# The order of score products inside a round: two halves of the array take the round's tiles in opposite order

## The chip, the cores and the metric

The kernel runs on one core of a Trainium2 chip. The metric is device time in microseconds from the start to the end of one launch: 2753.59 us, the median of three runs (2750.57 to 2754.35). A profile of one further execution, with a record of every instruction, goes with it. In it PE is the matrix engine TensorE, PEld its weight loads, DVE VectorE, ACT ScalarE, POOL GpSimd and SP the engine that issues transfers.

## What is computed

A pre-norm transformer layer on x of shape (4, 1024, 1024) in f32: attention with 32 heads of 32 elements and rotary positions, then a top-1 mixture of eight low-rank adapters. Only the scores matter here:

```
q = rotary(layernorm(x) @ wq);  k = rotary(layernorm(x) @ wk);  v = layernorm(x) @ wv
scores = einsum('bqhd,bkhd->bhqk', q, k) / sqrt(32)      # causal
out    = einsum('bhqk,bkhd->bqhd', softmax(scores), v)
x = x + out @ wo
x = x + adapter(layernorm(x))
```

Each score is a sum over the 32 elements of a head; because of the causal mask a block of queries needs only the keys up to itself.

## The kernel before

**Units.** Work goes through 32 units, one for each batch (4) and group of four heads (8). For a unit the queries and keys of its four heads lie in `qT` and `kT` with the 128 rows being head by element, so head h occupies rows 32h to 32h+31.

**Tiles of queries and rounds.** The 1024 queries of a unit are cut into 16 tiles t = 0 to 15 of 64 queries. Tile t needs the first (t+1)*64 keys. The tiles are computed in nine rounds, listed in `SLOTS` (lines 26 to 38) as (tile, first key, last key); two more entries of that list ("second", "first") are the places where the probabilities of a finished half are multiplied with the values. Four rounds hold one tile (15, 14, 13, 12), three hold two (7 and 6; 11 and a piece of 8; 10 and the rest of 8), one holds three (5, 4, 3) and one holds four (2, 1, 0 and 9).

**A round.** `score_round` (lines 393 to 423) fills one scores buffer `sc` of 128 rows by 4 heads by 512 columns; there is a single such buffer, and the value products use it too. The 128 rows are four strips of 32: strip i = 2*half + odd, where `half` says which 32 of the tile's 64 queries, and `odd` whether the strip takes the even or the odd blocks of 32 keys. Two strips together hold one set of queries, so a tile with K keys takes w = K/2 columns. Every (strip, head) pair is one product: 32 rows of one head as contraction, 32 queries as stationary operand, w keys as moving operand. It therefore uses one of the 16 squares of 32 by 32 of the matrix array: head h picks the array's rows, strip i the array's columns. A tile takes 16 products, one on each square, and the next tile of the round takes the same squares again.

The widths w by round are: 256+224; 192+160+128; 96+64+32+320; 512; 480; 448; 416; 384+128; 352+160.

**The order before.** For each tile of the round in the order of `SLOTS`, strips 0 to 3, and in a strip heads 0 to 3 (loops of lines 399, 402 and 404). So all 16 products of one tile stand ahead of the 16 of the next.

**After the products.** Lines 415 to 423: ScalarE copies each tile's scores into the probabilities' block `pr` (L417), GpSimd adds the causal mask on the diagonal (L420), VectorE finds the maxima (L438) and joins two strips (L459), ScalarE exponentiates (L467), VectorE transposes (L492). The value products `av` (L573) follow on eight squares of 64 by 32.

**What stands around a round.** The order of TensorE's instructions is written by hand (a manual schedule). Between rounds the kernel takes steps from a list `todo`: the projections of the next unit (`chain`, L313, matmuls of 128 by 128 by 512), and, from the second batch on, the output projection and the adapter of the batch before (L690, L712, L751). How many steps follow each round is set by costs and by `LENGTHS`, none of which the change touches.

Of the kernel before, what the change touches and what calls it, by code (L numbers as in the profile page):

```python
# [14 lines left out]
P = 128  # L15
# [4 lines left out]
SQ = 32  # L20
# [51 lines left out]
def tile_preln_attn_then_top1_lora(  # L72
# [78 lines left out]
    for i in range(P // SQ):  # L151
        half, odd = divmod(i, 2)
# [233 lines left out]
    def place(u, t):  # L386
        blk = t // QT
        if (u, blk) not in blocks:
            blocks[u, blk] = big.tile([P, HG, WIDTH[blk]], F32, tag=f"prob{blk}", name=f"pr_{u}_{blk}")
        at = (t % QT) * APART[blk]  # L390
        return blocks[u, blk][:, :, at : at + (t + 1) * SQ]

    def score_round(u, pieces):
        sc = ps_s.tile([P, HG, HALF], F32, tag="s", name=f"s_{u}_{pieces[0][0]}_{pieces[0][1]}")
        of_q = qTs[u].rearrange("p (j k) -> p j k", k=SQ)
        of_k = kTs[u].rearrange("p (j c k) -> p c j k", c=2, k=SQ)
        at = 0
        spans = []
        for t, k0, k1 in pieces:
            w = (k1 - k0) // 2  # L400

            for i in range(P // SQ):
                half, odd = divmod(i, 2)
                for h in range(HG):
                    rows = slice(h * HD, (h + 1) * HD)
                    nc.tensor.matmul(  # L406
                        sc[i * SQ : (i + 1) * SQ, h, at : at + w].rearrange("p (j k) -> p j k", k=SQ),
                        lhsT=of_q[rows, 2 * t + half],
                        rhs=of_k[rows, odd, k0 // (2 * SQ) : k1 // (2 * SQ)],
                        start=True,  # L410
                        stop=True,
                    )
            spans.append((t, k0 // 2, w, at))
            at += w
        for t, k0, w, at in spans:
            pr = places[u, t] if (u, t) in places else places.setdefault((u, t), place(u, t))
            nc.scalar.copy(pr[:, :, k0 : k0 + w], sc[:, :, at : at + w])  # L417
            if k0 + w == (t + 1) * SQ:
                diagonal = pr[:, :, t * SQ : (t + 1) * SQ]
                nc.gpsimd.tensor_tensor(  # L420
                    diagonal, diagonal, causal_sb.unsqueeze(1).to_broadcast([P, HG, SQ]), ALU.add
                )
                ended.append(t)
# [583 lines left out]
    for u, (b, g) in enumerate(units):  # L1007
# [10 lines left out]
        for r, pieces in enumerate(SLOTS):  # L1018
# [20 lines left out]
            else:  # L1039
                release_exps()  # L1040
                turn_probabilities()
                if second < r < first_:
                    join_sums(u, 0)
                score_round(u, pieces)
                if r == second - 1 and u:
                    while any((u - 1, t) in places for t in range(QT, 2 * QT)):
# [40 lines left out]
    left = sum(s.cost for s in todo) - APART_BY  # L1087
# [55 lines left out]
```

## Time and profile before

| what | value |
|---|---|
| median of three runs | 2753.59 us |
| the profiled execution, its time | 2747.7 us |
| its span, first to last instruction | 2745.9 us |
| mean granted TensorE clock | 0.998 |
| L406, score products: records, busy | 17408, 393.0 us |
| L406, weight loads: records, busy | 17408, 187.2 us |
| L573, value products: busy | 273.2 us |
| L313, projections pq, pk, pv: busy | 476.8, 475.9, 484.1 us |
| L417, ScalarE's copies of scores: busy, idle before | 525.3, 492.3 us |

How to read it: busy time is the union of the instructions of a group. Every f32 product leaves two matmul records and two weight-load records, so 8704 score products give 17408 of each. The length of a single matmul record reaches from its start to a modelled end; the products of one round overlap, so their lengths add up to far more than their busy time. "Idle before" is the time in which the group's engine stood still before its instructions.

### The profile page before, as it was taken

The page shows a single profiled execution, that of the slowest core. Times are in us where ns is not written, and L with a number is a line of the kernel's source. Part 1 is how long each engine was busy: PE and PEld are TensorE (multiplying, and loading weights), DVE is VectorE, ACT ScalarE, POOL GpSimd, SP SyncE. Part 2 cuts the span into 40 slices and gives each one's busy share as a digit, 9 for nine tenths or more (in the row PEclk, how much of TensorE's full clock was granted, in tenths as well). Part 3 has the DMA queues.
Part 4 walks back from the last instruction along what each step waited for, and adds up shares of the span by engine and source line. Part 5 has one row for each costly group of instructions (what it writes and reads, how often), then busy time and mean ns, then how long its engine had stood idle before and what let it go on. Part 6 is the DMA issues. An engine that isn't in the chain of part 4 may idle for free.

```text
span 2745.9 us, 84082 instructions
## 1 busy us (share of the span) xinstructions
PE 2682.2 (98%) x35328; PEld 1322.0 (48%) x35328; DVE 2126.7 (77%) x4198; ACT 1755.0 (64%) x5033; POOL 638.1 (23%) x900
## 2 busy tenths in 40 slices
PE   8999999899999999989999999998999999999998
PEld 5444444444445444445444454444544444544445
DVE  4888889887777877887777778788777777778655
ACT  2877777876666676666666666666566666666521
POOL 2222223222222222222222222222222222222000
PEclk9999999999999999999999999999999999999999
DMA  3222232325444455551654444565255544446421
GB/s 118 52 56 56 56 94 56 78 56 150 131 135 114 121 141 142 151 171 43 175 145 122 135 110 121 149 165 146 63 157 150 138 128 128 115 119 196 129 67 55
DMA packets 448012, 317.86 MB, mean 116 GB/s; under 512 B 150289, under 2 KB 371729, under 8 KB 447633
## 3 DMA queue, kind: packets, MB, share of 16 engines
q1 hardware_dynamic: 447632, 312.47, 41.6%
q8 instruction: 278, 4.55, 0.7%
q14 instruction: 102, 0.83, 0.1%
HBM read 262.59 MB, written 49.81 MB: 114 GB/s over the span
## 4 chain that ended last, share of the span: by engine, by line
PE 80%; DVE 14%; ACT 2%; DMA 1%; POOL 1%; issue 1%; SPq 0%; POOLq 0%; DVEq 0%; ACTq 0%
PE po L690 14%; PE pq L313 14%; PE pk L313 13%; PE pv L313 12%; PE s L406 11%; PE av L573 9%; DVE top L438 4%; DVE pr L492 4%; PE ph L712 2%; PE pf L751 2%; DMA chunk<-in_wo 1%; DVE both L459 1%; PE pr L547 1%; ACT pr L417 1%; PE pt_f L198 1%
## 5 line engine op out<-in xcount | busy, mean ns | idle before, releaser
L467 ACT ACTIVATE pr<-pr,both 128x256 f32<-128x256 f32 (+15 forms) x2048 | 1045.1, 519 | 58.0 <-DVE both L459 57.9
L438 DVE TENSOR_REDUCE top<-pr 128x2 f32<-128x960 f32 (+15 forms) x768 | 651.1, 894 | 251.5 <-POOL pr L420 250.9
L417 ACT COPY pr<-s 128x640 f32<-128x640 f32 (+14 forms) x544 | 525.3, 1017 | 492.3 <-PE s L406 491.7
L492 DVE STREAM_TRANSPOSE pr<-pr 128x1024 f32<-128x1024 f32 (+11 forms) x768 | 664.3, 907 | 33.3 <-ACT pr L467 30.1
L420 POOL TENSOR_TENSOR pr<-pr,causal_sb 128x128 f32<-128x128 f32 x512 | 238.0, 472 | 1070.6 <-ACT pr L417 1062.4
L313 PE MATMUL pv<-xnT,wv 128*128 128x512 f32 x1024 | 484.1, 600 | 0.0
L313 PE MATMUL pq<-xnT,wq 128*128 128x512 f32 x1008 | 476.8, 600 | 0.6 <-ACT xnT L200 0.6
L313 PE MATMUL pk<-xnT,wk 128*128 128x512 f32 x1008 | 475.9, 601 | 0.0
L406 PE MATMUL s<-kT,qT 32*32 32x256 f32 (+4 forms) x17408 | 393.0, 385 | 10.7 <-ACT pr L417 7.2
L467 ACT ACTIVATION_READ_ACCUMULATOR pr<-pr,both 128x1 f32 x2048 | 400.8, 196 | 0.0
L690 PE MATMUL po<-chunk,attn 128*128 128x512 f32 x736 | 376.3, 597 | 4.0 <-DMA chunk<-in_wo 4.0
L406 PEld LDWEIGHTS s<-kT,qT 32*32 32x32 f32 x17408 | 187.2, 103 | 267.2 <-issue 101.8
L313 PEld LDWEIGHTS pk<-xnT,wk 128*128 128x128 f32 x1008 | 181.3, 190 | 234.8 <-issue 234.6
L313 PEld LDWEIGHTS pq<-xnT,wq 128*128 128x128 f32 x1008 | 182.6, 191 | 224.0 <-issue 221.8
L313 PEld LDWEIGHTS pv<-xnT,wv 128*128 128x128 f32 x1024 | 185.7, 190 | 217.2 <-issue 212.9
L573 PE MATMUL av<-pr,vals 64*32 64x256 f32 (+3 forms) x12288 | 273.2, 320 | 11.7 <-DVE pr L492 11.6
L573 PEld LDWEIGHTS av<-pr,vals 64*32 64x32 f32 x12288 | 215.5, 106 | 119.9 <-issue 54.5
L459 DVE TENSOR_TENSOR both<-top 32x4 f32<-32x4 f32 (+3 forms) x1152 | 213.4, 185 | 23.7
L690 PEld LDWEIGHTS po<-chunk,attn 128*128 128x128 f32 x736 | 135.2, 190 | 168.0 <-issue 149.6
L548 ACT COPY by<-pr 128x512 f32<-128x512 f32 x64 | 37.5, 586 | 260.5 <-PE pr L547 260.5
L593 DVE TENSOR_TENSOR at<-av,by 128x256 f32<-128x256 f32 x128 | 48.1, 417 | 158.1 <-ACT by L548 158.0
L690 PE MATMUL po<-wo,attn 128*128 128x512 f32 x256 | 116.7, 597 | 0.0
(87 smaller groups left out, 1705.8 us busy)
## 6 DMA issues: line engine op xcount, KB each, us to landing
chunk<-in_wo SPq DMA_DIRECT2D x368, 256.0 KB, 3.6
vals<-vd SPq DMA_DIRECT2D x256, 128.0 KB, 4.5
x<-in_x SPq DMA_DIRECT2D x58, 512.0 KB, 6.0
wq<-in_wq SPq DMA_DIRECT2D x32, 512.0 KB, 4.0
wk<-in_wk SPq DMA_DIRECT2D x32, 512.0 KB, 4.0
wv<-in_wv SPq DMA_DIRECT2D x32, 512.0 KB, 4.2
vd<-vT SPq DMA_DIRECT2D x128, 128.0 KB, 4.8
out_y<-x SPq DMA_DIRECT2D x32, 512.0 KB, 2.8
```

The costliest lines, as they stand in the source:

```text
L313: nc.tensor.matmul(at["p"], lhsT=wt[:, c, :], rhs=xnTs[b, tb][:, c, :], start=(c == 0), stop=(c == NC - 1),)
L406: nc.tensor.matmul(sc[i * SQ : (i + 1) * SQ, h, at : at + w].rearrange("p (j k) -> p j k", k=SQ), lhsT=of_q[rows, 2 * t + half], rhs=of_k[ ...
L417: nc.scalar.copy(pr[:, :, k0 : k0 + w], sc[:, :, at : at + w])
L420: nc.gpsimd.tensor_tensor(diagonal, diagonal, causal_sb.unsqueeze(1).to_broadcast([P, HG, SQ]), ALU.add)
L438: nc.vector.tensor_reduce(top[:, k, h : h + step], places[u, t][:, h : h + step, :], AX.X, ALU.max, negate=True,)
L459: nc.vector.tensor_tensor(dst[rows], src[rows], src[other], op)
L467: nc.scalar.activation(pr[:, h, :], pr[:, h, :], AF.Exp, bias=tops[u, t][:, h : h + 1], accum_out=dens[u, t // QT][:, t % QT, h : h + 1],)
L492: nc.vector.transpose(pr, pr)
L573: nc.tensor.matmul(avs[half][h * HD : (h + 1) * HD, t0:, :], lhsT=v[rows, j, h * HD : (h + 1) * HD], rhs=rhs, start=(j == 0), stop=(j == n ...
L690: nc.tensor.matmul(st["po"], lhsT=lhsT, rhs=rhs, start=(c == start), stop=(c == stop))
L712: nc.tensor.matmul(ph, lhsT=st["ynT"][:, c, :], rhs=w[:, c - i * RA, :], start=(c == 0), stop=(c == NC - 1),)
L751: nc.tensor.matmul(pf, lhsT=st["whT"], rhs=rhs, start=True, stop=True)
```

## The change

The products of a round are the same; their order is another. The array's columns are taken as two halves, half 0 (strips 0 and 1) and half 1 (strips 2 and 3). Half 0 has a list of the round's tiles from the widest to the narrowest, half 1 from the narrowest to the widest. The code takes eight products at a time (two strips by four heads) from one of the two lists: from the half whose count of columns so far, plus 64 for each group taken, is the smaller one; half 0 at a tie. A round of 384+128 so becomes: 384 on half 0, 128 on half 1, 384 on half 1, 128 on half 0.

Where each tile's columns stand in `sc`, the copies after the products and their order remain. The slice of keys is written in another way, for the same keys (k0 and w now count half-columns).

```diff
         for t, k0, k1 in pieces:
             w = (k1 - k0) // 2
-
-            for i in range(P // SQ):
-                half, odd = divmod(i, 2)
+            spans.append((t, k0 // 2, w, at))
+            at += w
+
+
+        left = [sorted(spans, key=lambda p: -p[2]), sorted(spans, key=lambda p: p[2])]
+        busy = [0, 0]
+        while left[0] or left[1]:
+            half = 0 if left[0] and (not left[1] or busy[0] <= busy[1]) else 1
+            t, k0, w, at = left[half].pop(0)
+            busy[half] += w + 2 * SQ
+            for odd in range(2):
+                i = 2 * half + odd
                 for h in range(HG):
                     rows = slice(h * HD, (h + 1) * HD)
                     nc.tensor.matmul(
                         sc[i * SQ : (i + 1) * SQ, h, at : at + w].rearrange("p (j k) -> p j k", k=SQ),
                         lhsT=of_q[rows, 2 * t + half],
-                        rhs=of_k[rows, odd, k0 // (2 * SQ) : k1 // (2 * SQ)],
+                        rhs=of_k[rows, odd, k0 // SQ : (k0 + w) // SQ],
                         start=True,
                         stop=True,
                     )
-            spans.append((t, k0 // 2, w, at))
-            at += w
```

The groups of eight come out in this order (width, half):

| round | order of groups |
|---|---|
| 256+224 | 256 h0, 224 h1, 256 h1, 224 h0 |
| 192+160+128 | 192 h0, 128 h1, 160 h1, 160 h0, 192 h1, 128 h0 |
| 96+64+32+320 | 320 h0, 32 h1, 64 h1, 96 h1, 96 h0, 320 h1, 64 h0, 32 h0 |
| one tile | h0, h1 |
| 384+128 | 384 h0, 128 h1, 384 h1, 128 h0 |
| 352+160 | 352 h0, 160 h1, 352 h1, 160 h0 |

## The prediction

> **What bounds the kernel now.** I read the page's engine shares first, then its chain of waits, then the group that the change touches, then single rounds in the timeline.
>
> ```profile
> PE 2682.2 (98%) x35328; PEld 1322.0 (48%) x35328; DVE 2126.7 (77%) x4198; ACT 1755.0 (64%) x5033; POOL 638.1 (23%) x900
> ...
> PE 80%; DVE 14%; ACT 2%; DMA 1%; POOL 1%; issue 1%; SPq 0%; POOLq 0%; DVEq 0%; ACTq 0%
> ...
> L406 PE MATMUL s<-kT,qT 32*32 32x256 f32 (+4 forms) x17408 | 393.0, 385 | 10.7 <-ACT pr L417 7.2
> ```
>
> TensorE is busy for 98% of the span and the chain of what ended last runs through it for 80%. The score products (L406) hold 393 us of it and are almost never kept waiting (10.7 us). So time added to or taken from a score round on TensorE goes to the end nearly in full; the scalar engine's 491.7 us of waiting for these rounds is slack, not cost.
>
> Next, one round with one tile (width 480) and one with two (widths 384 and 128), weight loads (PEld) and products (PE), from the timeline: start us, length us, engine, names, count, idle before.
>
> ```profile
> 1056.86 0.23 PEld L406 LDWEIGHTS s<-kT,qT 32*32 32x32 f32 x32 [0.76 <-ACT pr L467]
> 1057.87 0.30 PEld L313 LDWEIGHTS pq<-xnT,wq 128*128 128x128 f32 x2 [0.79 <-issue]
> ```
>
> ```profile
> 1001.48 0.46 PEld L406 LDWEIGHTS s<-kT,qT 32*32 32x32 f32 x33 [0.76 <-PE po L690]
> 1002.16 0.55 PEld L406 LDWEIGHTS s<-kT,qT 32*32 32x32 f32 x31 [0.22 <-issue]
> 1002.91 0.19 PEld L313 LDWEIGHTS pv<-xnT,wv 128*128 128x128 f32 x1 [0.20 <-issue]
> ```
>
> A product shows two weight loads and two matmuls (two passes over its columns), so a tile's 16 products make 32 loads. In the second round the loads stop after number 33 and resume after a pause that nothing in the profile explains ("issue"). How many score matmuls are in flight in 10 ns slices of that round (PE count, then PEld count):
>
> ```profile
> 1001.93:1001.94 0.01, 0.01 (x32) 0.01 (x1) 1.00 1.62 614
> 1002.30:1002.31 0.01, 0.01 (x17) 0.00 (x0) 1.00 0.00 0
> 1002.40:1002.41 0.01, 0.01 (x8) 0.01 (x7) 1.00 0.00 0
> 1002.60:1002.61 0.01, 0.01 (x24) 0.01 (x12) 1.00 2.62 205
> ```
>
> The reader sees 32 in flight, then a hole around 1002.40, then a slow refill. That hole is the cost of every round with more than one tile.
>
> From the start times and lengths of the single records I get these rules. Products on different tiles of the array start 6.7 ns apart. A pass over w columns streams for w/1.2 ns (each one-tile round that is 32 columns narrower is 53 ns shorter, twice 26.7), with 24 ns ahead of the first pass for the weights, 2.5 ns between passes, and 160 ns from the end of the stream to completion: product 1 of width 384 is complete at 24+320+2.5+320+160 = 827 ns. [...] A later one comes in when the one 16 places ahead is complete, *in program order*: product 17 trickles in by parts, product 18's load starts 31 ns after product 1 is complete (seen at 858 ns), and each further product 16.7 ns after the one before. The next foreign matmul starts 71 ns ahead of the last completion. Entry by entry this gives, in ns from a round's first product to the next foreign matmul: 1067, 1014, 960, 907 for the four one-tile rounds (measured 1071, 1017, 965, 911), 1364 for widths 256+224 (1371), 1566 for 192+160+128 (1575), 1832 for 96+64+32+320 (1841), 1418 for 384+128 (1424), 1418 for 352+160 (1424). The same rules place the starts of both passes on the first tile of a value block (L573, eight tiles) within 5 ns for its first six widths. All nine kinds of round, then, by one set of rules, none off by more than 9 ns.
>
> [...]
>
> **The change part by part.** It adds, removes and resizes no instruction; DVE, ACT, POOL and SP keep their counts and order. ACT's first copy of a round starts after the whole round (at 1003.02 for the round that left TensorE at 1002.91), so which tile is finished first is worth nothing. Only the order of the 16 to 64 products inside a round changes, in groups of eight (left half of the array's columns, right half).
>
> One-tile rounds: eight left, eight right, as before: 0.
>
> 256+224 becomes 256 left, 224 right, 256 right, 224 left. Product 1 is complete at 614, product 18 enters at 645, product 24 at 745, product 32 at 879. The last 224-wide one needs 24+187+2.5+187+160 = 560 and sets the end; the 256-wide number 24 is done earlier. Same end: 0.
>
> 192+160+128 becomes 192, 128, 160, 160, 192, 128. The middle window is all 160 as before, and the last group is 128-wide and enters last: 0.
>
> 384+128 becomes 384 left, 128 right, 384 right, 128 left. Product 18 enters at 858, as before, since product 1 is still 384 wide. But products 17 to 24 now are 384 wide: number 24 enters at 858+6x16.7 = 958 and takes 827, so 1785. Before, the last was a 128-wide one, entering at 858+14x16.7 = 1092 and taking 24+107+2.5+107+160 = 400, so 1492. That is +293 ns.
>
> 352+160: number 24 enters at 803+100 = 903 and takes 773, so 1676, against 1489 before: +187 ns. In both, half of the widest products used to be in the first window, in parallel with the other half; now half of them starts when the first half is complete.
>
> 96+64+32+320 becomes 320, 32, 64, 96, 96, 320, 64, 32. Before, the narrow tiles turn the window over quickly and 320 comes last, all 16 at once. After, the first window is not free until product 1 (320) is complete at 720; the second holds 64 and 96 on the same half; the second 320 group enters from 1178 to 1348 and is complete by 2063; and the last eight narrow ones, behind it in program order, come in only from about 1920 on and end at 2318, against 1903 before: +414 ns.
>
> Sum per unit (one batch and one group of four heads): 187+293+414 = 894 ns; 32 units: 28.6 us.
>
> What hides some of it: in the first eight units TensorE waits 0.9 us for ACT's copy of the 352+160 round, which by then stands behind exponentials; 7 times 0.19 = 1.3 us is absorbed. The rest of TensorE's idle time after the start is either one-off or follows from TensorE's own results. Net +27.3 us. The profiled execution took 2747.7 us (span 2745.9, 1.8 around it): 2775.0, or +0.99%. On the median shown, 2753.6, that is 2781 us. What I cannot see in the trace of before is a window with two widths in one tiling stage; from below the cost is bounded at about 20 us (the four-tile round's term halved, if its last groups slip in earlier), from above at 36 us (knock-on waits of ACT and DVE of some 0.25 us a unit).
>
> **The rivals.** (1) The pause is a tile that is still busy: product 17 returns to tile 0 while that is streaming. For it: product 17 does start just as tile 0 comes free (667 ns at width 384). Then beginning with the narrow half helps: at 384+128 that half is free by 53+24+2x107 = 291 instead of 667, at 352+160 by 344 instead of 614, the three-tile round may gain some 0.2 us, and the four-tile round is level; (0.37+0.27+0.2) x 32 = 27 us faster, 2727 us. At most all excess over a full array could go: 0.35+0.56+0.77+0.35+0.35 = 2.4 us a unit, 76 us. Against it: product 18's tile is idle from about 674, yet its load waits until 858, and the value products revisit busy tiles without a pause. (2) No effect, 2753.6: entries freed in any order, or the longer rounds lie beside waits of equal length. Against it: refill follows the slowest pass of product 1, though the first passes of all others are long complete; and TensorE idles 64 us in all, 11 of them at the start, before any round. (3) Slower by more, 2800 us: rounds that end later delay the maxima and exponentials until the scores' buffer is not free for the next round; 0.4 us more on two rounds of half of the units is 13 to 20 us on top. Against it: only 7.2 us of such waits now.
>
> **How the numbers follow.** Forecast 0.86 (its own range 2773 to 2790), rival 1 0.06, rival 2 0.04, rival 3 0.04. A measurement here tells 0.2% (5.5 us) from nothing. Faster 0.06, same 0.04, slower 0.90. Range 2769 to 2791.
>
> **What would show it.** In the changed trace: rounds 384+128 at about 1.71 us, 352+160 at 1.60, four-tile at 2.25, the other six as before; L406's busy time near 393+28 us; the other engines' sums unchanged. A 384+128 round no longer than 1.42 us, or loads that run on past number 33 without a pause, would make it wrong.

## The result and the profile after

The changed kernel takes 2773.05 us (median of six runs, 2769.88 to 2778.6) against 2753.14 us for the kernel before in the same comparison. The ratio is 1.0082, with a 95% interval of 1.0071 to 1.0093: slower by 22.6 us, between 19.5 and 25.6 (the two medians alone differ by 19.9). That is well outside the 0.2% that a measurement tells from nothing.

In the listing of the changed kernel everything after the new loop stands seven lines lower: score products are L415 (before L406), ScalarE's copies L424 (L417). The page after, engine shares and the group of the score products:

```profile
PE 2712.1 (98%) x35328; PEld 1331.7 (48%) x35328; DVE 2125.5 (77%) x4198; ACT 1756.4 (63%) x5033; POOL 640.2 (23%) x900
...
PE 81%; DVE 14%; ACT 2%; POOL 1%; issue 1%; DMA 1%; POOLq 0%; SPq 0%; ACTq 0%; DVEq 0%
...
L415 PE MATMUL s<-kT,qT 32*32 32x256 f32 (+4 forms) x17408 | 420.9, 386 | 7.4 <-ACT pr L424 4.5
```

The counts are those of before, and DVE, ACT and POOL are busy for the same time within 2 us or so. TensorE is busy 29.9 us longer, of which 27.9 us are the score products (420.9 after 393.0). They wait even less than before (7.4 us after 10.7). So the time comes from inside the rounds, not from a new wait. The timeline of the 384+128 round that was shown of before:

```profile
1006.84 0.29 PEld L415 LDWEIGHTS s<-kT,qT 32*32 32x32 f32 x33 [0.76 <-PE po L697]
1006.85 1.79 PE L415 MATMUL s<-kT,qT 32*32 32x384 f32 x64
1007.38 0.10 PEld L415 LDWEIGHTS s<-kT,qT 32*32 32x32 f32 x1 [0.24 <-issue]
1007.70 0.36 PEld L415 LDWEIGHTS s<-kT,qT 32*32 32x32 f32 x30 [0.22 <-issue]
1008.56 0.70 PE L313 MATMUL pv<-xnT,wv 128*128 128x512 f32 x1
```

The same 33 loads come first, although the records of the eight narrow products among them end 0.50 us into the round. One more load follows, and then the other 30 start at 1007.70, 0.86 us after the round began, as before (858 ns there, inside the second row shown). But from here the eight wide products of the other half still have their whole way to go: the next projection starts at 1008.56, 1.72 us after the round's first product instead of 1.42. The number of score matmuls in flight in 10 ns slices of this round:

```profile
1007.28:1007.29 0.01, 0.01 (x24) 0.00 (x0) 1.00 1.15 205
1007.48:1007.49 0.01, 0.01 (x9) 0.00 (x1) 1.00 0.53 205
1007.65:1007.66 0.01, 0.01 (x9) 0.00 (x0) 1.00 1.97 410
1007.75:1007.76 0.01, 0.01 (x6) 0.01 (x6) 1.00 0.53 205
1008.20:1008.21 0.01, 0.01 (x24) 0.00 (x0) 1.00 1.05 410
```

The count drops to 9 by 1007.48, and nothing new comes in for 0.2 us although half of the array is empty: as I read these counts and the order of the list, the places are held by narrow products that are complete but stand behind a wide one (experiments 6 and 7 test this). The four-tile round in the timeline after (the projection that follows starts at 1051.28):

```profile
1049.02 0.23 PEld L415 LDWEIGHTS s<-kT,qT 32*32 32x32 f32 x33 [0.76 <-issue]
1049.51 0.10 PEld L415 LDWEIGHTS s<-kT,qT 32*32 32x32 f32 x1 [0.25 <-issue]
1049.78 1.01 PEld L415 LDWEIGHTS s<-kT,qT 32*32 32x32 f32 x80 [0.17 <-issue]
1050.96 0.29 PEld L415 LDWEIGHTS s<-kT,qT 32*32 32x32 f32 x14 [0.17 <-issue]
1051.28 0.70 PE L697 MATMUL po<-chunk,attn 128*128 128x512 f32 x1
```

The row of loads stops early behind the wide group at its head, and again at 1050.8 behind the second wide group; the last 14 loads, of seven narrow products, come in only at 1050.96. By the starts of the single records two loads that follow each other stand 356 ns apart at the first pause and 269 at the last; before, in the same unit, 170 ns at most.

The length of a round from its first product to the next foreign matmul, taken from the starts of the single records, as a median over the 32 units of one profiled execution, in ns (a few single rounds are longer; the last section has the longest):

| round | before | after | difference | predicted difference |
|---|---|---|---|---|
| 256+224 | 1371 | 1371 | 0 | 0 |
| 192+160+128 | 1575 | 1575 | 0 | 0 |
| 96+64+32+320 | 1841 | 2260 | +419 | +414 |
| 384+128 | 1424 | 1717 | +293 | +293 |
| 352+160 | 1424 | 1611 | +187 | +187 |
| four one-tile rounds, each | 1072 to 911 | 1072 to 911 | 0 or 1 | 0 |

### The profile page after: what moved, and what is told of

It reads as the page before. It is cut to its first block, busy times and chain, and to the rows that moved or that the text cites. A ratio compares the mean times of both kernels' runs of the same rounds, so it can differ in the third digit from the quotient of the medians.

```text
span 2768.1 us, 84082 instructions
## 1 busy us (share of the span) xinstructions
PE 2712.1 (98%) x35328; PEld 1331.7 (48%) x35328; DVE 2125.5 (77%) x4198; ACT 1756.4 (63%) x5033; POOL 640.2 (23%) x900
## 4 chain that ended last, share of the span: by engine, by line
PE 81%; DVE 14%; ACT 2%; POOL 1%; issue 1%; DMA 1%; POOLq 0%; SPq 0%; ACTq 0%; DVEq 0%
PE po L697 15%; PE pq L313 14%; PE pk L313 13%; PE pv L313 12%; PE s L415 12%; PE av L580 8%; DVE top L445 4%; DVE pr L499 4%; PE ph L719 2%; PE pf L758 2%; DVE both L466 1%; PE pr L554 1%; ACT pr L424 1%; PE pt_f L198 1%; ACT pr L474 1%
## 5 line engine op out<-in xcount | busy, mean ns | idle before, releaser
L424 ACT COPY pr<-s 128x640 f32<-128x640 f32 (+14 forms) x544 | 525.5, 1018 | 524.8 <-PE s L415 524.2
L415 PE MATMUL s<-kT,qT 32*32 32x256 f32 (+4 forms) x17408 | 420.9, 386 | 7.4 <-ACT pr L424 4.5
L415 PEld LDWEIGHTS s<-kT,qT 32*32 32x32 f32 x17408 | 196.3, 103 | 282.9 <-issue 121.2
```

The source lines that it names most:

```text
L415: nc.tensor.matmul(sc[i * SQ : (i + 1) * SQ, h, at : at + w].rearrange("p (j k) -> p j k", k=SQ), lhsT=of_q[rows, 2 * t + half], rhs=of_k[ ...
```

## The experiments

In what follows "window theory" means the rule of the prediction: 16 products are in the array at once, and a new one gets its place only when the one 16 places ahead in program order is complete. In the traces of before and after no round of the 288 in each has more than 32 score matmuls, two a product, in flight. In the 384+128 round shown of before, product 1's records end at 827 ns, a modelled time, and product 18's first load starts at 858; with 352, 256, 192 and 96 columns at the head it starts at 805, 645, 538 and 378 ns (medians). In the 384+128 round shown of after it starts at 859 ns, although the narrow products' records end at 0.50 us. No record shows a place being freed: the rule is an estimate from these starts and lengths. All experiments are built on the kernel before, with the products of a round written as a list of (strip, tile) from which four products each are issued. Round lengths are medians as in the table above:

```
        for i, n in order:
            t, k0, w, at = spans[n]
            for h in range(HG):
                ...
```

**1. The change only where the theory gives nothing.**

```diff
+        if widths in ((256, 224), (192, 160, 128)):
...
+        else:
+            order = [(i, n) for n in range(len(spans)) for i in range(P // SQ)]
```

> The new order only in the rounds 256+224 and 192+160+128, the order of before in all others. Window theory (16 products in the array, freed in program order on completion): these two rounds stay at 1.37 and 1.58 us, no other round moves, time within 0.2% of before. Rival 'the order by halves costs by itself' (for instance because the half of the array is switched every eight products): some 20 to 30% longer here too, 0.3 us each and about +19 us in all. Rival 'busy tile': both rounds shorter by 0.1 to 0.2 us, some -6 us.

Measured: both rounds at 1371 and 1575 ns, all others as before; ratio 1.0003 (0.9994 to 1.0012). Alternating the halves of the array costs nothing by itself, and it gains nothing by finding a free tile. Both rivals of this run fall.

**2. The change only in the two unequal two-tile rounds** (the same edit, for widths (384, 128) and (352, 160)).

> The new order only in the rounds 384+128 and 352+160. Window theory: those rounds 1.71 and 1.60 us instead of 1.42, all others as before, 32 x 0.48 = 15.4 us of TensorE time added; with the share that waits have absorbed in the changed kernel (22.6 of 28.8 us arrived) about +11 to +15 us. If what is absorbed lies in the first eight units, where TensorE waits for the copy of the 352+160 round, this part loses more than the four-tile part. Rival 'the time comes from waits on ACT and DVE and not from the rounds themselves': round lengths as before and TensorE's waits longer.

Measured: 1717 and 1611 ns, all others as before; ratio 1.0036 (1.0023 to 1.0049), which is +9.9 us (6.3 to 13.5) of the 15.4 us added in the rounds. The point estimate lies just below the expected 11 to 15, the interval reaches into it. The waits for the scores' copy fell from 7.2 to 4.3 us, so the rival, time from longer waits, falls.

**3. The change only in the four-tile round** (the same edit, for rounds of four tiles).

> The new order only in the four-tile round 96+64+32+320. Window theory: that round 2.26 us instead of 1.84, all others as before, 32 x 0.42 = 13.4 us of TensorE time added, +10 to +13 us in the time. Together with the kernel that has the new order only in the rounds 384+128 and 352+160 it gives the whole change. Rival 'the parts work together' (later ends of several rounds pile up in the scores' buffer): the two parts alone add up to clearly less than the 20 to 23 us of the whole.

Measured: that round 2263 ns, all others within 2 ns of before; ratio 1.0033 (1.0022 to 1.0043), +9.1 us (6.0 to 11.8) of 13.4; this too lies below what was expected, 10 to 13, with the interval reaching into it. Experiment 2 was to lose more of its sum than this one if the hiding lay in the first eight units; it lost 5.5 us and this one 4.3, which the intervals don't tell apart. The two parts add to 19.0 us; the whole is 22.6. With intervals of some 3 us on each that is no clear difference, so the data don't call for a joint effect.

**4. An order made from the theory.** In the rounds of two and four tiles: narrow products first on part of the strips, the widest together on all four, the rest last; in the three-tile round the widest stand in two pairs. Tiles are numbered as they stand in the round, and the lists follow from the rules of the prediction:

```diff
+        if len(spans) == 2:
+            order = [(0, 1), (1, 1), (2, 0), (3, 0), (0, 0), (1, 0), (2, 1), (3, 1)]
+        elif len(spans) == 3:
+            order = [(1, 2), (2, 1), (0, 0), (3, 0), (0, 1), (1, 1), (3, 2), (2, 2), (2, 0), (1, 0), (3, 1), (0, 2)]
+        elif len(spans) == 4:
+            order = [(1, 2), (3, 1), (2, 3), (1, 3), (3, 3), (0, 3), (2, 0), (1, 0)]
+            order += [(0, 1), (2, 1), (3, 2), (0, 2), (3, 0), (0, 0), (1, 1), (2, 2)]
```

> An order worked out from the window theory: the narrow products of a round on some strips first, so that the first places come free early, then the widest on all four strips, then the rest. Window theory: rounds 256+224 at 1.32 us (1.37 before), 192+160+128 at 1.48 (1.58), 96+64+32+320 at 1.74 (1.84), 384+128 and 352+160 at 1.35 (1.42 both): 0.41 us a unit, 13 us less TensorE time, time 9 to 13 us shorter than before. Rival 'busy tile' or 'any order that isn't tile by tile costs': no round shorter than before, time the same or longer.

Measured: 1318, 1482, 1743, 1345 and 1345 ns; ratio 0.9961 (0.9947 to 0.9976), 10.7 us faster than before (6.6 to 14.6). This order beats both kernels. Its 384+128 round in the timeline:

```profile
996.17 1.15 PEld L415 LDWEIGHTS s<-kT,qT 32*32 32x32 f32 x64 [0.76 <-PE po L697]
996.17 1.42 PE L415 MATMUL s<-kT,qT 32*32 32x128 f32 x64
997.51 0.70 PE L313 MATMUL pv<-xnT,wv 128*128 128x512 f32 x1
```

All 64 loads stand in one row of 1.15 us: by the window theory the narrow products at the head give their places back so early that no pause is long enough to part the row. The page of this kernel has TensorE at 2671.9 us busy:

```profile
PE 2671.9 (98%) x35328; PEld 1338.3 (49%) x35328; DVE 2129.9 (78%) x4198; ACT 1754.3 (64%) x5033; POOL 636.9 (23%) x900
```

**5. The change mirrored:** each half takes its tiles the other way round, so that the narrow group stands first.

```diff
-            by_width = sorted(range(len(spans)), key=lambda n: - spans[n][2])
+            by_width = sorted(range(len(spans)), key=lambda n: spans[n][2])
```

(The line removed is that of experiments 1 to 3; half 0 takes `by_width`, half 1 the same list from its end, in all rounds of more than one tile.)

> The change mirrored in all rounds of more than one tile: half 0 takes the tiles from the narrowest to the widest, half 1 from the widest to the narrowest, so the same alternation of halves with the narrow group first. Window theory: 256+224 at 1.32 us (1.37 before), 192+160+128 at 1.49 (1.58), 384+128 and 352+160 at 1.35 (1.42), only the four-tile round longer, 2.11 (1.84), since its wide group stands between narrow ones; sum over a unit -0.02 us, time within 0.3% of before. Rival 'alternating halves cost by themselves': the same round lengths as with the change (1.72 and 1.61 for 384+128 and 352+160), about +20 us.

Measured: 1318, 1495, 2116, 1344 and 1344 ns; ratio 0.9999 (0.9991 to 1.0008). The same alternation of halves, begun on the narrow side, makes four of the five rounds shorter than before and only the four-tile round longer. So what matters is which products stand ahead in the window, not that halves alternate.

**6 and 7. Program order or not.** In the two unequal two-tile rounds the first sixteen products are four wide ones and twelve narrow ones, each on its own square of the array in both kernels; only the place of the four wide ones in the list differs. The second sixteen are the same. Going from list 6 to list 7 (only in these two rounds; the score products are L410 here):

```diff
-            order = [(0, 0), (1, 1), (2, 1), (3, 1), (0, 1), (1, 0), (2, 0), (3, 0)]
+            order = [(1, 1), (2, 1), (3, 1), (0, 0), (0, 1), (1, 0), (2, 0), (3, 0)]
```

> Only the rounds 384+128 and 352+160 changed: four wide products on strip 0 first, then twelve narrow ones on strips 1 to 3, then four narrow ones on strip 0 and twelve wide ones. Window theory with freeing in program order: 384+128 takes 1.85 us, 352+160 1.75. Freeing in any order, or by tile: no difference from the kernel with the same groups where the four wide ones stand behind the twelve narrow ones.

> As the kernel before it, but the four wide products on strip 0 stand behind the twelve narrow ones of the first sixteen; the second sixteen are the same in the same order. Window theory with freeing in program order: 384+128 takes 1.73 us, 352+160 1.63, each 0.12 us shorter than with the wide ones first. Any other freeing: the same as with the wide ones first.

Measured: 1852 and 1745 ns with the wide ones first, 1732 and 1625 with them behind the narrow ones. Each is 120 ns shorter, as worked out. Both are lengths of one execution each; no times are compared. The timeline of a 384+128 round, wide ones first:

```profile
1005.26 0.46 PEld L410 LDWEIGHTS s<-kT,qT 32*32 32x32 f32 x33 [0.76 <-PE po L692]
1005.93 0.55 PEld L410 LDWEIGHTS s<-kT,qT 32*32 32x32 f32 x31 [0.22 <-issue]
1007.11 0.70 PE L313 MATMUL pv<-xnT,wv 128*128 128x512 f32 x1
```

and wide ones last of the sixteen:

```profile
1003.66 0.23 PEld L410 LDWEIGHTS s<-kT,qT 32*32 32x32 f32 x32 [0.76 <-PE po L692]
1004.10 0.68 PEld L410 LDWEIGHTS s<-kT,qT 32*32 32x32 f32 x32 [0.20 <-issue]
1005.40 0.70 PE L313 MATMUL pv<-xnT,wv 128*128 128x512 f32 x1
```

With the narrow ones ahead the second half of the loads begins 0.44 us into the round; with a wide one ahead a single load comes at 0.67 us and the rest only from 0.86. The sets of products, and the squares that they use, are the same in both. Were places freed in any order, or by square, list 7 could gain only from its narrow products' starting earlier, 27 ns at most (an estimate: four starts of 6.7 ns), and its wide ones start later; freeing in program order gives the 120.

**8. The change only in the first eight units** (the whole change, under `if u < 8`).

> The change only in the first eight units, the order of before in the other 24. Rounds add 8 x 0.90 = 7.2 us of TensorE time. If waits for ACT in these units absorb most of it, as the traces before and after suggest (unit 8 begins 1.8 us later after the change), unit 8 begins 1 to 3 us later than before and the time is within 0.1% of before. If what is absorbed is spread evenly over all units: unit 8 begins 5 to 6 us later and the time is 0.2% longer.

Measured: ratio 1.0015 (1.0008 to 1.0021), which is +4.1 us (2.2 to 5.8) for 7.2 us added in the rounds; unit 8 begins at 609.8 us, 2.6 later than in the profile before. The start of unit 8, of a single execution, is as expected if the hiding lies in these units (1 to 3) and not as for an even spread (5 to 6); the time lies between the two cases and leaves the share open. The profiles below say more of it.

## Why the prediction was right, point by point

**The bound.** Right in the main: what was added inside the rounds is in TensorE's busy time, and some four fifths of it in the end. The forecast was +27.3 us and 2781 us; measured were +22.6, with 25.6 as the upper end, and 2773.05, at the very edge of the narrower range, 2773 to 2790, which so held by a hair. The miss is in the term for what is hidden, below.

**The window.** Right, as the cause and in its sizes. The three terms of the sum were +293, +187 and +414 ns and measured +293, +187 and +419; the six rounds that were to stay did. Per unit that is 899 ns for 894, over 32 units 28.8 us for 28.6. Experiments 4 to 7 take the same rules to orders that no trace had shown, and every round comes out within 6 ns of the length written down for it beforehand.

**The rivals.** A busy tile (rival 1) would have made experiment 1 faster, and list 7 no shorter than list 6, since product 17 returns to the square of a wide one in both; neither happened. In the trace of list 7 the narrow products at places 17 to 20 start only 749 ns into the round, when the wide ones ahead have left their squares, while wide ones behind them in the list start from 487 ns on: a busy square held up its own product alone. Freeing in any order (rival 2) falls with 6 and 7, by their 120 ns. A pile-up behind the scores' buffer (rival 3) would lengthen L415's waits for ACT; they went from 7.2 to 4.5 us.

**What was hidden.** Here a size was off. I put 1.3 us of the sum beside waits; by the medians 28.8 us were added in the rounds and 22.6 arrived, so 3 to 9 us were hidden by the interval of the times. In the two profiles the rounds, summed record by record, differ by only 27.2 us, since before the change more four-tile rounds stood still (last section), and the spans differ by 22.2: about 5.0 us were hidden there. By stretches of eight units, TensorE first, before:

```profile
62.85:607.23 544.38, 520.54 (x8061) 249.87 (x8060) 465.04 (x908) 421.66 (x1217) 151.47 (x215) 0.99 0.26 62
607.23:1278.18 670.95, 663.00 (x8781) 323.77 (x8780) 528.65 (x1042) 439.42 (x1263) 158.51 (x224) 1.00 0.49 133
1278.18:1953.56 675.38, 667.45 (x8809) 326.78 (x8808) 530.13 (x1048) 438.58 (x1257) 159.03 (x224) 1.00 0.48 133
```

and after:

```profile
63.23:608.99 545.76, 526.23 (x8061) 251.48 (x8060) 465.34 (x909) 422.27 (x1218) 151.57 (x215) 0.99 0.25 62
608.99:1285.73 676.74, 670.06 (x8780) 325.99 (x8779) 527.53 (x1041) 439.43 (x1261) 159.19 (x223) 1.00 0.47 131
1285.73:1968.79 683.06, 676.37 (x8809) 329.60 (x8808) 530.18 (x1048) 439.14 (x1257) 159.50 (x224) 1.00 0.47 131
```

The score rounds of these stretches are longer by 5.6, 7.1 and 7.4 us in the sum of their records. The first stretch grew by 1.4 us, the second by 5.8, the third by 7.7. So most of the hiding, 4.2 us, is in the first eight units, where the step "7 times 0.19" stands. Two rounds with the wait behind them, before:

```profile
180.47 1.49 PE L406 MATMUL s<-kT,qT 32*32 32x384 f32 x64
184.67 1.49 PE L406 MATMUL s<-kT,qT 32*32 32x352 f32 x64
190.71 1.44 PE L406 MATMUL s<-kT,qT 32*32 32x256 f32 x64 [0.92 <-ACT pr L417]
```

and after:

```profile
181.30 1.79 PE L415 MATMUL s<-kT,qT 32*32 32x384 f32 x64
185.79 1.68 PE L415 MATMUL s<-kT,qT 32*32 32x352 f32 x64
191.55 1.44 PE L415 MATMUL s<-kT,qT 32*32 32x256 f32 x64 [0.45 <-ACT pr L424]
```

The wait shrank by 0.47 us: the 0.19 that I counted, and the 0.29 of the 384+128 round too. I had taken ACT's late copy to follow from the end of that round. But the exponentials that stand ahead of the copy start 5.78 us after the round's start in both profiles:

```profile
186.25 0.64 ACT L467 ACTIVATE pr<-pr,both 128x416 f32<-128x416 f32 x1 [2.32 <-DVE both L459]
```

```profile
187.08 0.64 ACT L474 ACTIVATE pr<-pr,both 128x416 f32<-128x416 f32 x1 [1.90 <-DVE both L466]
```

They are those of the tile before (416 wide) and wait for its maxima on VectorE, so a longer 384+128 round only eats into the wait. Two other runs show the same: in experiment 6 the two rounds are 0.75 us longer than before, in experiment 3 they are as before, and the wait is

```profile
189.52 1.44 PE L410 MATMUL s<-kT,qT 32*32 32x256 f32 x64 [0.17 <-ACT pr L419]
```

```profile
192.31 1.44 PE L418 MATMUL s<-kT,qT 32*32 32x256 f32 x64 [0.92 <-ACT pr L427]
```

The trace before has six such waits (units 2 to 7), not seven, and together they fell from 7.2 to 4.5 us: 2.7 us instead of the 1.3 that I counted. The rest, some 2 us, I can place only in part: the transposes of x (pt_a) waited 3.4 us for ACT instead of 5.2, and other groups of TensorE differ by up to 1.7 us either way between the two executions.

## What to carry to other kernels

In these runs sixteen f32 products of 32 by 32 fit in at once (32 matmuls in flight at most, in the traces of before and after), and the starts fit a wide product at the head holding the places of every narrow one behind it until it was complete: loads went on in number only 0.86 us into a round with 384 columns at the head (before, after, experiment 6), and 0.44 us with 128 there (list 7). So when small products run side by side on squares of the array, read how many fit in and look at what stands at the head. The order that won here (1345 ns instead of 1424 at 384+128) issues some narrow products first, so that, by that reading, places come free early, then, in the rounds of two and four tiles, all the widest ones side by side, and ends with narrow ones. What lost was a wide tile split in two groups: experiment 5's four-tile round, with narrow groups between the two, took 2116 ns instead of 1841. Narrow ones first are not enough: list 7 begins with twelve of them and takes 1732 ns instead of 1424, as most of its wide ones come last. Other types and shapes were not run. A measure of how much work each half has been given says nothing of this; the starts of the weight loads, with the pauses between them, do.

## What the runs showed beyond that

In each of these profiles a four-tile round stands still for 0.6 to 2.1 us with nothing in the profile to release it; before and after the change it is that of unit 2. This differs from run to run and makes two single profiles differ by a microsecond or more where no instruction has changed. It may not be independent of the order: in the five profiles whose four-tile rounds all have the order of before (before, 1, 2, 6, 7) six to nine further ones are 0.1 to 0.2 us longer, and the pauses add to 2.5 to 4.1 us; in the four with another order (after, 3, 4, 5) there is at most one of these, and the sum is 0.6 to 1.8 us. The cause was not looked for, and each is a single execution.
